# The first 256 tokens in two parts of 128, and the last silu in two halves with GpSimd beside VectorE

## The chip, the cores and the metric

The kernel runs on one core of a Trainium2 chip. The core has five engines that each work through their own queue in order: TensorE (PE in the profile; its weight loads are listed as PEld), VectorE (DVE), ScalarE (ACT), GpSimd (POOL) and SyncE (SP), which here only issues DMAs. They wait for each other through semaphores. The metric is the device time of one execution in microseconds (us), as the median of several runs. The kernel before takes 820.97 us (median of 3 runs, 820.76 to 821.0).

## What is computed

All is float32. `x` has 4 sequences of 1024 tokens, each token with 1024 features: 4096 rows. The reference, cut to what matters here:

```python
xn = _layernorm(x)                                   # per token: (x - mean) / sqrt(var + eps)

# first branch: a gate, and a recurrence along the sequences
g   = sigmoid(xn @ gate_w.T + gate_b)
u_g = xn * g
d_eff = d + mean_over_tokens(u_g) @ d_lr_u @ d_lr_v / rank
s   = c * decayed_cumsum(b * u_g) + d_eff * u_g

# second branch: three layers, and the top 2 of 8 routes
route = top2(softmax(xn @ wr.T))
h = silu(xn @ w1.T)
h = silu(h @ w3.T)
h = h @ w2.T
out = zeros_like(xn)
for k in range(2):
    out = out.at[index[:, k]].add(gate[:, k] * h)    # index is a route: rows 0 to 7 alone
g = silu(out)

return x + s * g
```

The rows that routes are added to are only rows 0 to 7 of `out`; silu of zero is zero, so all rows of the result but the first eight are `x` itself. The eight rows need a sum over all tokens of `h`, weighted by the gates, which is why all three big products (w1, gate_w for the first tokens, w3) are computed and w2 is applied once, at the very end, to the eight sums.

## The kernel before

**Tiles.** Tokens are taken in four super-blocks of 1024 (`sb`). For a super-block a product such as `xn @ w1.T` is a 1024 x 1024 x 1024 product. It is done as a 2 x 2 block product with seven block products in place of eight (a Strassen-Winograd scheme): the seven are numbered 1 to 7 and each of them is itself split once more in the same way into seven small products. A small product (`small`) is four matmuls with a 128 x 128 weight tile and 256 moving columns, accumulated in PSUM in two column halves. The class `Half` holds one of the block products, and its `step(n)` issues its n-th small product into one of the banks X, Z or Y and then has VectorE or ScalarE carry the bank into the result (`first`, `more`, `whole`). The kinds are "u" (w1), "g" (gate_w, only needed for the first super-block) and "m" (w3).

**The first product.** The first "u" product (line 211, `plain`) is done without the scheme: eight small products, two for each quarter of its result, since the sums that the scheme needs aren't there yet. The first "g" product uses the scheme. `at_first` (line 1438) says how the steps of the two are interleaved: steps 0 and 1 of "u" (bank X_u), then 0 and 3 of "g" (banks X_g and Y_g), then on with "u". These four small products need only the first 256 tokens of `xn`, the first half of the w1 block and the first half of the gate_w block.

**Normalisation of the first tokens.** `xT`, the transposed input, has features on the partitions, so mean and scale of a token have to lie along the free axis, the same on all partitions. `first_tokens` (line 317) takes the moments of tokens 0 to 255 from `x` itself (`x_first`, four pieces of 128 tokens by 512 features; VectorE's BN_STATS and BN_AGGREGATE), makes 128 x 128 diagonal matrices of the means (`spread(0, ...)`) and of the scales (`spread(1, ...)`), and multiplies them on TensorE by a matrix of ones, which puts each token's mean (bank mean_00) and scale (bank scale_00) on all partitions. `scales` computes the reciprocal root with one Newton step. Then `on` subtracts the mean and multiplies by the scale, on VectorE, straight in the tile of `xT`. `warm` issues matmuls on constants, whose results nobody reads, so that TensorE is at work meanwhile (`IDLE` of them ahead of everything). For the other quarters of the super-block (tokens 256 to 511 and so on) `stats0` and `norm0` do the same with larger operations; the mean and scale of tokens 256 to 511 go to bank acc.

**What sets the order.** Every engine instruction is pinned to the order in which the program issues it. This order is written by hand as places on a line: `at(place, f)` puts a function at a place, a generator may `yield` a distance to its next part, and before each small product at its place all that is due by then is issued. So a changed place moves instructions relative to those of the same engine, TensorE's queue among them: `stats0(0, 1, ..., 11.9, apart=1)` at place -8 puts the matmuls for mean and scale of tokens 256 to 511 at 3.9 and 4.9, between small products at 3, 4 and 5.

**DMAs.** All loads of the start go through SP's queue but two pieces of `x_first`, which ACT issues. The order on SP: two pieces of x, the first xT piece, the first half of w1's block, the second xT piece, the first half of gate_w's block, then x for tokens 256 to 511, the second halves, the rest of xT. Each DMA uses one of eight semaphores in turn; a DMA waits until the one eight before it has landed.

**The end.** After the last product, `the_rest` sums the last gated rows, transposes them, multiplies them by w2 into bank pp (32 partitions for each of four groups of 256 features, of which 8 rows are used), and then applies silu on ScalarE, multiplies by `y` and adds `x` on VectorE, each as one instruction of 128 x 256, and stores four pieces of 8 x 256, two by SP and two by ACT.

Of the kernel before, what the change touches and what calls it, by code (L numbers as in the profile page):

```python
# [10 lines left out]
F32 = mybir.dt.float32  # L11
I32 = mybir.dt.int32
U32 = mybir.dt.uint32
AF = mybir.ActivationFunctionType
# [8 lines left out]
def kernel(  # L23
# [99 lines left out]
                self.home.append(self.tile)  # L123

    NB, NQ = 20, 18
    IDLE = 14
    blocks = deque(
        const.tile([P, 4, 2 * Q], F32, tag=f"b{i}", name=f"b{i}") for i in range(NB)
    )
# [18 lines left out]
    pool.memset(three_halves, 1.5)  # L148

    x_first = block()  # L150
    for n in range(2):
        for t, queue in ((0, sync), (1, act)):
            queue.dma_start(
                x_first[:, 2 * t + n, :], x[t * P : (t + 1) * P, n * H : (n + 1) * H]
            )

    root = const.tile([P, 1], F32, tag="root", name="root")
    act.activation(root, eps, AF.Sqrt)
# [83 lines left out]
    def part(t, a):  # L242
        return t[:, 2 * a : 2 * a + 2, :].rearrange("p b (k n) -> p (b k) n", n=Q)
# [3 lines left out]
    def stats0(I, a, xb, lag, wait=(0, 0), apart=0):  # L247

        mv = sp.tile([P, 2, 2], F32, tag="mv", name=f"mv_{I}{a}")
        for tt in range(2):  # L250
            xt = xb[:, 2 * tt : 2 * tt + 2, :]
            bn = sp.tile([P, 2, nc.vector.BN_STATS_DIM], F32, tag=f"bn{tt}", name=f"bn_{I}{a}{tt}")
            for n in range(2):
                dve.bn_stats(bn[:, n, :], xt[:, n, :])
            dve.bn_aggr(mv[:, tt, :], bn)
        xb.drop()
        dg = quarter()

        def diagonals(s, w):
            for tt in range(2):  # L260
                act.activation(
                    dg[:, (2 * s + tt) * P : (2 * s + tt + 1) * P],
                    ident,
                    AF.Identity,
                    scale=w[:, tt : tt + 1],
                )

        if (I, a) == (1, 1):
            bc = ps_sm.tile([P, 2, Q], F32, tag="sm", name="bc_11")
        elif (I, a) == (1, 0):  # L270
            bc = ps_y.tile([P, 2, Q], F32, tag="Y", name="bc_10")
        else:
            bc = acc.rearrange("p (s n) -> p s n", s=2)
        yield wait[0]

        sd, v, r1 = (bc[:, 1, 2 * i : 2 * i + 2] for i in range(3))
        act.activation(sd, mv[:, :, 1], AF.Sqrt, bias=eps)
        act.activation(v, mv[:, :, 1], AF.Identity, bias=eps)
        diagonals(0, mv[:, :, 0])
        r0 = sp.tile([P, 2], F32, tag="r2", name="r0")  # L280
        rs = sp.tile([P, 2], F32, tag="rs", name=f"rs_{I}{a}")
        dve.reciprocal(r0, sd)
        dve.reciprocal(r1, sd)
        dve.scalar_tensor_tensor(rs, r0, -0.5, r1, ALU.mult, ALU.mult)
        dve.tensor_mul(rs, rs, v)
        dve.scalar_tensor_tensor(rs, rs, 1.5, r1, ALU.add, ALU.mult)
        yield wait[1]
        diagonals(1, rs)
        yield lag
        for s in range(2):  # L290
            if s:
                yield apart
            pe.matmul(
                bc[:, s, :],
                ones,
                dg[:, s * Q : (s + 1) * Q],
                start=True,
                stop=True,
                skip_group_check=True,
            )  # L300
            bc0[I, a] = [bc[:, s, :] for s in range(2)]
        dg.drop()

    def norm0(I, a, J, apart=0):
        p = part(xn[0, I, J], a)
        for s, op in ((0, ALU.subtract), (1, ALU.mult)):
            if s and apart:
                yield apart
            row = bc0[I, a][s].unsqueeze(1).to_broadcast([P, 4, Q])
            dve.tensor_tensor(p, p, row, op)  # L310

    def warm(n):

        for _ in range(n):
            pe.matmul(idle, ones, ident, start=True, stop=True, skip_group_check=True)

    def first_tokens():


        mv = sp.tile([P, 2, 2], F32, tag="mv", name="mv_00")  # L320
        bn = [
            sp.tile([P, 2, nc.vector.BN_STATS_DIM], F32, tag=f"bn{t}", name=f"bn_00{t}")
            for t in range(2)
        ]
        for n in range(2):
            for t in range(2):
                dve.bn_stats(bn[t][:, n, :], x_first[:, 2 * t + n, :])
        for t in range(2):
            dve.bn_aggr(mv[:, t, :], bn[t])
        x_first.drop()  # L330
        sd = sp.tile([P, 2], F32, tag="sd2", name="sd_00")
        act.activation(sd, mv[:, :, 1], AF.Sqrt, bias=eps)
        dg = quarter()
        rows = [
            ps_acc.tile([P, Q], F32, tag="rows", name="mean_00"),
            ps_sm.tile([P, Q], F32, tag="sm", name="scale_00"),
        ]
        bc0[0, 0] = rows

        def spread(s, w):  # L340
            d = dg[:, s * Q : (s + 1) * Q]
            for t in range(2):
                dve.tensor_scalar(
                    d[:, t * P : (t + 1) * P], ident, w[:, t : t + 1], None, ALU.mult
                )
            pe.matmul(rows[s], ones, d, start=True, stop=True, skip_group_check=True)

        spread(0, mv[:, :, 0])
        warm(2)
        v = sp.tile([P, 2], F32, tag="v2", name="v_00")  # L350
        dve.tensor_scalar(v, mv[:, :, 1], EPS, None, ALU.add)
        rs = sp.tile([P, 2], F32, tag="rs", name="rs_00")
        scales(rs, v, sd, 2)
        spread(1, rs)
        dg.drop()
        warm(3)
        p = part(xn[0, 0, 0], 0)

        def on(lo, hi, s, op):
            row = rows[s].unsqueeze(1).to_broadcast([P, hi - lo, Q])  # L360
            dve.tensor_tensor(p[:, lo:hi, :], p[:, lo:hi, :], row, op)

        on(0, 2, 0, ALU.subtract)
        on(0, 1, 1, ALU.mult)
        on(1, 2, 1, ALU.mult)
        on(2, 4, 0, ALU.subtract)
        on(2, 4, 1, ALU.mult)

    def stats(sb, bcs):

# [219 lines left out]
    def first_sums(t):  # L590

        for _ in fresh_sums("g", 1, t, False):
            yield 0.5
        yield 3
        for _ in left_sums("u", 0, 1, 1):
            yield 0.5

# [313 lines left out]
    class Half:  # L911
# [33 lines left out]
        def step(self, n):  # L945
# [16 lines left out]
            elif n == 0:  # L962
                go(self.X, A[:, 0], t[:, 0], True, False)
                self.first(0, self.X)
            elif n == 1:
                go(self.Z, s[0].tile, ts[0].tile, True, False)
                self.first(3, self.Z)
                s[0].drop()
                ts[0].drop()
            elif n == 2:  # L970
                go(self.X, s[1].tile, ts[1].tile, False, False)
                self.first(1, self.X)
                s[1].drop()
                ts[1].drop()
            elif n == 3:
                Y = ps_y.tile([P, 2 * Q], F32, tag="Y", name=f"Y_{self.tag}")
                go(Y, A[:, 1], t[:, 2], True, True)
                if (self.kind, self.i) == ("g", 1):
                    at(Y_AT, self.more, 0, Y)
                else:  # L980
                    self.more(0, Y)
            elif n == 4:
                go(self.X, s[2].tile, ts[2].tile, False, False)
                self.more(3, self.X)
                s[2].drop()
                ts[2].drop()
            elif n == 5:
                go(self.Z, s[3].tile, t[:, 3], False, True)
                self.more(1, self.Z)
                s[3].drop()  # L990
            elif n == 6:
                go(self.X, A[:, 3], ts[3].tile, False, True)
                self.first(2, self.X)
                self.whole(2)
                ts[3].drop()
# [237 lines left out]
    sync.dma_start(first[:, 0, :], xT[0, 0, 0, :, 0, :])  # L1233
    first_half("w1", 0)
    sync.dma_start(first[:, 1, :], xT[0, 0, 0, :, 1, :])
    first_half("gw", 0)
    load_x0(0, 1)
    first_half("w1", 1)
# [7 lines left out]
    at(-16, load_xn, 0, 1, 0, USES[1, 0] + G[1, 0])  # L1246
    at(-15, load_xn, 0, 1, 1, USES[1, 1] + G[1, 1])
    at(-10, first_tokens)
    at(-8, lambda: stats0(0, 1, x0[0, 1], 11.9, apart=1))
    at(3.95, norm0, 0, 1, 0, 1)  # L1250
    at(6, lambda: stats0(1, 0, x0[1, 0], 2.5, (1.5, 1)))
    at(6.5, norm0, 0, 0, 1)
    at(8.5, norm0, 0, 1, 1)
# [4 lines left out]
    at(18, norm0, 1, 1, 1)  # L1258
    at(26, consts)
    for IJ in HB:  # L1260
        at(0, lambda IJ=IJ: left.__setitem__(("u", 0, IJ), xn[(0,) + IJ]))

    halves = []
    for kind, sb, i, plain in line:
# [117 lines left out]
    def the_rest():  # L1382
# [36 lines left out]
            dve.tensor_add(accT[:, 4 + 2 * b : 6 + 2 * b, 0:E], ta[:, ks, :], half[:, ks, :])  # L1419
            part_out((4 + 2 * b, 5 + 2 * b), False, b == 0)  # L1420
        o = fin["o"]
        act.activation(o, p, AF.Silu)
        dve.tensor_mul(o, o, fin["y"])
        dve.tensor_add(o, o, fin["x"])
        for w in range(4):
            (sync, act)[w % 2].dma_start(
                out[0:E, w * Q : (w + 1) * Q], o[CG * w : CG * w + E, :]
            )

# [13 lines left out]
        (at_first[kind, sb, i][n] if (kind, sb, i) in at_first else start[kind, sb, i] + 2 * n, k, n)  # L1443
        for k, (kind, sb, i, plain) in enumerate(line)
        for n in range(8 if plain else 7)
    )
    for place, k, n in steps:
        here[0] = place
# [81 lines left out]
```

## Time and profile before

| what | value |
|---|---|
| median of 3 runs | 820.97 us (820.76 to 821.0) |
| the profiled execution | 820.79 us |
| its span, first to last instruction | 819.0 us |
| PE busy | 811.4 us (99%), 4087 matmul records |
| DVE, ACT, POOL busy | 510.6, 267.3, 496.5 us |
| mean granted TensorE clock | 0.999 |
| DMA moved | 192.88 MB, mean 235 GB/s |
| first matmul of X_u | 10.32 us |
| last matmul of pp ends | 814.81 us |

The span runs from the first to the last instruction; what lies around it (1.8 us) is in the time of the execution and not in the profile. All instructions that go through the class `Pinned` are listed under its line 89, so the profile is read by the names of the tiles: `X_u<-b,b` is a matmul that writes bank X_u of a "u" product from two large tiles, `q` is a tile of 128 x 512, `b` one of 128 x 2048, `bn` and `mv` are moments. A name followed by "q" (SPq, ACTq) is the engine's queue, here the issuing of a DMA. Busy shares are averages over the whole span: the start up to 10 us and the tail from 805 us are a small part of them.

### The profile page before, as it was taken

How to read it: one execution, taken by the hardware profiler on the slowest of the kernel's cores; microseconds unless marked ns; L12 is line 12 of the kernel's file. 1: busy time of each engine (PE TensorE's matmuls, PEld its weight loads, DVE VectorE, ACT ScalarE, POOL GpSimd, SP SyncE). 2: the span in 40 equal slices, each digit the busy share in tenths (PEclk: the TensorE clock that was granted, in tenths of full speed). 3: DMA queues.
4: the chain of work that ended last, by engine and by line, in shares of the span. 5: the costliest groups of instructions: out<-in, count | busy, mean ns of one | idle time of the engine just before them, and what ended most of it. 6: DMA issues, size and time to landing. Idle time of an engine off the chain costs nothing.

```text
span 819.0 us, 11323 instructions
## 1 busy us (share of the span) xinstructions
PE 811.4 (99%) x4087; PEld 698.2 (85%) x4087; DVE 510.6 (62%) x872; ACT 267.3 (33%) x470; POOL 496.5 (61%) x398
## 2 busy tenths in 40 slices
PE   8999999999999999999999999999999999999997
PEld 7888888888888878888888788888888788888885
DVE  6986598765588534764985235666983246667643
ACT  2345126877233237341022065421122021220111
POOL 2799796957999394644547453754448454465300
PEclk9999999999999999999999999999999999999999
DMA  9946609464978958629955866559766355555700
GB/s 341 423 169 232 231 27 359 180 244 152 409 275 311 339 183 295 246 88 380 387 170 221 334 224 238 193 206 385 282 244 241 120 213 207 197 177 178 302 14 2
DMA packets 55927, 192.88 MB, mean 235 GB/s; under 512 B 6480, under 2 KB 9792, under 8 KB 44224
## 3 DMA queue, kind: packets, MB, share of 16 engines
q1 hardware_dynamic: 55552, 191.61, 63.6%
q8 instruction: 33, 0.54, 0.2%
q10 hardware_dynamic: 320, 0.54, 0.2%
q14 instruction: 22, 0.18, 0.1%
HBM read 169.01 MB, written 39.87 MB: 255 GB/s over the span
## 4 chain that ended last, share of the span: by engine, by line
PE 98%; DMA 1%; DVE 0%; issue 0%; SPq 0%; ACT 0%
PE X_u L89 24%; PE X_m L89 24%; PE Z_u L89 12%; PE Z_m L89 12%; PE Y_m L89 6%; PE X_g L89 6%; PE Y_u L89 6%; PE Z_g L89 3%; PE acc L89 2%; PE plT L89 2%; PE Y_g L89 1%; DMA b<-in_x 1%; PE pp L89 0%; PE bc L89 0%; DVE bn L89 0%; PE accB L89 0%
## 5 line engine op out<-in xcount | busy, mean ns | idle before, releaser
L89 POOL TENSOR_TENSOR q<-b 128x512 f32<-128x512 f32 x154 | 203.5, 1336 | 194.6 <-PE X_m L89 48.0
L89 ACT ACTIVATE b<-b 128x512 f32<-128x512 f32 (+1 forms) x152 | 105.4, 696 | 296.5 <-DVE b L89 292.5
L89 POOL TENSOR_TENSOR q<-b,q 128x512 f32<-128x512 f32 x98 | 133.7, 1368 | 7.2 <-issue 4.0
L89 POOL TENSOR_TENSOR b<-b,b 128x512 f32<-128x512 f32 x72 | 93.1, 1318 | 48.5 <-PE X_u L89 33.8
L89 DVE TENSOR_TENSOR b<-b,b 128x512 f32<-128x512 f32 x120 | 109.2, 924 | 2.7
L89 PE MATMUL X_m<-q,q 128*128 128x256 f32 x448 | 105.9, 379 | 0.0
L89 PE MATMUL X_u<-q,q 128*128 128x256 f32 x432 | 102.4, 380 | 0.0
L89 DVE TENSOR_TENSOR b<-X_u,b 128x512 f32<-128x512 f32 x87 | 60.1, 691 | 58.6 <-PE X_u L89 57.9
L89 DVE TENSOR_TENSOR b<-X_m,b 128x512 f32<-128x512 f32 x88 | 60.3, 687 | 56.9 <-PE X_m L89 56.6
L89 PEld LDWEIGHTS X_m<-q,q 128*128 128x128 f32 x448 | 85.0, 190 | 12.4 <-issue 0.8
L89 POOL TENSOR_TENSOR q<-q,b 128x512 f32<-128x512 f32 x56 | 73.7, 1317 | 32.3 <-PE X_u L89 25.1
L89 PEld LDWEIGHTS X_u<-q,q 128*128 128x128 f32 x432 | 81.8, 190 | 12.2 <-issue 1.2
L89 DVE TENSOR_TENSOR b<-b,bc 128x1024 f32<-128x1024 f32 x56 | 67.8, 1210 | 0.1
L89 PE MATMUL X_u<-b,b 128*128 128x256 f32 x248 | 58.4, 379 | 0.0
L89 PE MATMUL Y_m<-b,b 128*128 128x256 f32 x224 | 53.1, 380 | 0.0
L89 PE MATMUL Z_m<-b,q 128*128 128x256 f32 x224 | 53.0, 379 | 0.0
L89 PE MATMUL X_m<-b,b 128*128 128x256 f32 x224 | 52.9, 379 | 0.0
L89 PE MATMUL Z_m<-q,q 128*128 128x256 f32 x224 | 52.9, 379 | 0.0
L89 PE MATMUL X_m<-q,b 128*128 128x256 f32 x224 | 52.9, 379 | 0.0
L89 PEld LDWEIGHTS X_u<-b,b 128*128 128x128 f32 x248 | 47.0, 190 | 6.4
L89 DVE TENSOR_TENSOR b<-Z_u,b 128x512 f32<-128x512 f32 x47 | 32.5, 691 | 31.6 <-PE Z_u L89 30.9
L89 PE MATMUL Z_u<-q,q 128*128 128x256 f32 x216 | 51.1, 379 | 0.0
(182 smaller groups left out, 1179.2 us busy)
## 6 DMA issues: line engine op xcount, KB each, us to landing
q<-w SPq DMA_DIRECT2D x168, 256.0 KB, 4.5
b<-in_w SPq DMA_DIRECT2D x36, 1024.0 KB, 8.8
b<-w_T SPq DMA_DIRECT2D x24, 1024.0 KB, 6.2
b<-in_xT SPq DMA_DIRECT2D x15, 1024.0 KB, 11.6
w<-q SPq DMA_DIRECT2D x56, 256.0 KB, 7.1
b<-in_x SPq DMA_DIRECT2D x12, 1024.0 KB, 10.9
w_T<-b SPq DMA_DIRECT2D x8, 1024.0 KB, 4.4
b<-in_gw SPq DMA_DIRECT2D x6, 1024.0 KB, 15.6
```

The source lines that it names most:

```text
L89: r = f(*args, **kwargs)
```

## The change

The first 256 tokens are handled in two parts of 128, each with its own moments, spreading, row operations and the four small products with 128 moving columns in place of 256; the DMAs of `x` are reordered so that the pieces of tokens 0 to 127 come first (one on SP, one on ACT) and those of tokens 128 to 255 later on SP; the diagonals of the means and the sum of variance and eps move from VectorE to ScalarE. The matmuls for mean and scale of tokens 256 to 511 and the row operations on them move by one place, and the second of the row operations is halved. At the end the silu is done in two halves of 128 columns, GpSimd multiplies and adds for the first and VectorE for the second, and of the four stores SP issues two, ACT one and GpSimd's queue one. The diff, cut (removed bodies of `first_tokens` are left out, they stand in the listing above; `urgent` is never set):

```diff
-    IDLE = 14
+    IDLE = 12
...
-    for n in range(2):
-        for t, queue in ((0, sync), (1, act)):
-            queue.dma_start(
-                x_first[:, 2 * t + n, :], x[t * P : (t + 1) * P, n * H : (n + 1) * H]
-            )
+    def first_piece(queue, t, n):
+        queue.dma_start(x_first[:, 2 * t + n, :], x[t * P : (t + 1) * P, n * H : (n + 1) * H])
+
+    first_piece(sync, 0, 0)
+    first_piece(act, 0, 1)
...
     def norm0(I, a, J, apart=0):
-            row = bc0[I, a][s].unsqueeze(1).to_broadcast([P, 4, Q])
-            dve.tensor_tensor(p, p, row, op)
+            n = 2 if s and apart else 4
+            row = bc0[I, a][s].unsqueeze(1).to_broadcast([P, n, Q])
+            for k in range(0, 4, n):
+                dve.tensor_tensor(p[:, k : k + n], p[:, k : k + n], row, op)
...
     def first_tokens():
+        def moments(t):
+            for n in range(2):
+                dve.bn_stats(bn[t][:, n, :], x_first[:, 2 * t + n, :])
+            dve.bn_aggr(mv[:, t, :], bn[t])
+            act.activation(sd[:, t : t + 1], mv[:, t, 1:2], AF.Sqrt, bias=eps)
+            act.activation(diagonal(0, t), ident, AF.Identity, scale=mv[:, t, 0:1])
+            act.activation(v[:, t : t + 1], mv[:, t, 1:2], AF.Identity, bias=eps)
+            o = slice(t, t + 1)
+            scales(rs[:, o], v[:, o], sd[:, o], 1)
+            dve.tensor_scalar(diagonal(1, t), ident, rs[:, o], None, ALU.mult)
...
+        hu.begin()
+        hg.begin()
+        moments(0)
+        spread(0, 0)
         warm(2)
+        spread(1, 0)
+        warm(2)
+        Y = ps_y.tile([P, 2 * Q], F32, tag="Y", name="Y_g0_1")
+        four = (
+            (hu.X, 0, hu.t[:, 0], True, False),
+            (hu.X, 1, hu.t[:, 2], False, True),
+            (hg.X, 0, hg.t[:, 0], True, False),
+            (Y, 1, hg.t[:, 2], True, True),
+        )
+        on(0, 2, 0, 0)
+        on(0, 1, 0, 1)
+        on(1, 2, 0, 1)
+        on(2, 4, 0, 0)
+        on(2, 4, 0, 1)
+        for n, (ps, q, B, start, stop) in enumerate(four):
+            half_small(ps, hu.A[:, q], B, 0, start, stop)
+            if n == 0:
+                moments(1)
+        x_first.drop()
+        spread(0, 1)
+        spread(1, 1)
         dg.drop()
+        for k in range(4):
+            for s in range(2):
+                on(k, k + 1, 1, s)
+        for ps, q, B, start, stop in four:
+            half_small(ps, hu.A[:, q], B, 1, start, stop)
+        at(3.9, hu.first, 0, hu.X)
+        at(3.9, hg.first, 0, hg.X)
+        at(Y_AT, hg.more, 0, Y)
...
-        yield 3
+        yield 3.6
         for _ in left_sums("u", 0, 1, 1):
...
     sync.dma_start(first[:, 1, :], xT[0, 0, 0, :, 1, :])
+    first_piece(sync, 1, 0)
+    first_piece(sync, 1, 1)
     first_half("gw", 0)
...
-    at(-8, lambda: stats0(0, 1, x0[0, 1], 11.9, apart=1))
-    at(3.95, norm0, 0, 1, 0, 1)
+    at(-8, lambda: stats0(0, 1, x0[0, 1], 12.9, apart=1))
+    at(4.96, norm0, 0, 1, 0, 1)
...
-        at(0, lambda IJ=IJ: left.__setitem__(("u", 0, IJ), xn[(0,) + IJ]))
+        at(-11, lambda IJ=IJ: left.__setitem__(("u", 0, IJ), xn[(0,) + IJ]))
...
         o = fin["o"]
-        act.activation(o, p, AF.Silu)
-        dve.tensor_mul(o, o, fin["y"])
-        dve.tensor_add(o, o, fin["x"])
+        for n, eng in ((0, pool), (1, dve)):
+            c = slice(n * P, (n + 1) * P)
+            act.activation(o[:, c], p[:, c], AF.Silu)
+            eng.tensor_mul(o[:, c], o[:, c], fin["y"][:, c])
+            eng.tensor_add(o[:, c], o[:, c], fin["x"][:, c])
         for w in range(4):
-            (sync, act)[w % 2].dma_start(
+            (sync, act, pool)[w % 3].dma_start(
                 out[0:E, w * Q : (w + 1) * Q], o[CG * w : CG * w + E, :]
             )
...
         for n in range(8 if plain else 7)
+        if not (k == 0 and n in (0, 1) or k == 1 and n in (0, 3))
```

In the new `first_tokens`, `on(lo, hi, t, s)` is the row operation (s = 0 subtracts the mean, s = 1 multiplies by the scale) on rows `lo` to `hi` of the tile and on part t, `spread(s, t)` is the 128-column matmul with the matrix of ones, and `half_small` issues the four matmuls of `small` with the 128 columns of part t. The last line takes the four steps, which `first_tokens` now issues itself, out of the list of steps.

More of the change, by code (lines that the diff above doesn't have):

```diff
@@ L257, in stats0, with diagonals @@
         dg = quarter()
-        def diagonals(s, w):
+        def diagonals(s, w, urgent=False):
             for tt in range(2):
[L261 to L266, printed above, removed]
+                d = dg[:, (2 * s + tt) * P : (2 * s + tt + 1) * P]
+                if urgent:
+                    dve.tensor_scalar(d, ident, w[:, tt : tt + 1], None, ALU.mult)
+                else:
+                    act.activation(d, ident, AF.Identity, scale=w[:, tt : tt + 1])
         if (I, a) == (1, 1):
@@ L278, in stats0 @@
         act.activation(v, mv[:, :, 1], AF.Identity, bias=eps)
-        diagonals(0, mv[:, :, 0])
+        diagonals(0, mv[:, :, 0], False)
         r0 = sp.tile([P, 2], F32, tag="r2", name="r0")
@@ L317, in first_tokens @@
     def first_tokens():
-        mv = sp.tile([P, 2, 2], F32, tag="mv", name="mv_00")
         bn = [
@@ L324, in first_tokens @@
         ]
[L325 to L330, printed above, removed]
+        mv = sp.tile([P, 2, 2], F32, tag="mv", name="mv_00")
         sd = sp.tile([P, 2], F32, tag="sd2", name="sd_00")
-        act.activation(sd, mv[:, :, 1], AF.Sqrt, bias=eps)
+        v = sp.tile([P, 2], F32, tag="v2", name="v_00")
+        rs = sp.tile([P, 2], F32, tag="rs", name="rs_00")
         dg = quarter()
@@ L338, in first_tokens @@
         bc0[0, 0] = rows
[L340 to L348, printed above, removed]
-        warm(2)
-        v = sp.tile([P, 2], F32, tag="v2", name="v_00")
-        dve.tensor_scalar(v, mv[:, :, 1], EPS, None, ALU.add)
@@ L352, in first_tokens @@
-        rs = sp.tile([P, 2], F32, tag="rs", name="rs_00")
-        scales(rs, v, sd, 2)
-        spread(1, rs)
-        dg.drop()
[L356 to L367, printed above, removed]
+        p = part(xn[0, 0, 0], 0)
@@ new lines, in first_tokens, with diagonal @@
+        hu, hg = halves[0], halves[1]
+        def diagonal(s, t):
+            n = s * Q + t * P
+            return dg[:, n : n + P]
+        def moments(t):
[8 more added lines that the diff above has]
+            dve.tensor_scalar(diagonal(1, t), ident, rs[:, o], None, ALU.mult)
@@ new lines, in spread, with on @@
+        def spread(s, t):
+            pe.matmul(
+                rows[s][:, t * P : (t + 1) * P],
+                ones,
+                diagonal(s, t),
+                start=True,
+                stop=True,
+                skip_group_check=True,
+            )
+        def on(lo, hi, t, s):
+            c = slice(t * P, (t + 1) * P)
+            row = rows[s][:, c].unsqueeze(1).to_broadcast([P, hi - lo, P])
+            op = (ALU.subtract, ALU.mult)[s]
+            dve.tensor_tensor(p[:, lo:hi, c], p[:, lo:hi, c], row, op)
@@ new lines, in half_small @@
+        def half_small(ps, A, B, t, start, stop):
+            for mt in range(2):
+                for kt in range(2):
+                    n = kt * Q + t * P
+                    pe.matmul(
+                        ps[:, mt * Q + t * P : mt * Q + (t + 1) * P],
+                        B[:, kt * Q + mt * P : kt * Q + (mt + 1) * P],
+                        A[:, n : n + P],
+                        start=(start and t == 0 and mt == 0 and kt == 0),
+                        stop=(stop and t == 1 and mt == 1 and kt == 1),
+                        skip_group_check=True,
+                    )
@@ new lines, in first_tokens @@
+        hu.begin()
+        hg.begin()
+        moments(0)
+        spread(0, 0)
+        warm(2)
+        spread(1, 0)
[6 more added lines that the diff above has]
+            (Y, 1, hg.t[:, 2], True, True),
+        )
+        on(0, 2, 0, 0)
+        on(0, 1, 0, 1)
+        on(1, 2, 0, 1)
+        on(2, 4, 0, 0)
@@ L977, in step @@
                 go(Y, A[:, 1], t[:, 2], True, True)
[L978 to L981, printed above, removed]
+                self.more(0, Y)
             elif n == 4:
```

## The prediction

> **What bounds the kernel now.** I read the chain of waits first, for the whole run (its shares by engine, the first line below) and then in order of time for its first 45 us (start, length, work): it says which work sets the end.
>
> ```profile
> PE 98%; DMA 1%; DVE 0%; issue 0%; SPq 0%; ACT 0%
> ...
> 1.20 4.66 DMA b<-in_x
> 5.86 0.02 issue
> 5.88 1.29 DVE bn L89 x2
> ...
> 9.80 0.67 PE idle L89 x6
> 10.47 3.57 PE X_u L89 x16
> ```
>
> PE is the bound from the first X_u to the tail. Between 10.3 and 813.7 us the trace has no moment in which PE stands still, so a microsecond won or lost at the start arrives at the end whole. Ahead of X_u stand the landing of x, the moments on DVE, and the spreading of mean and scale. Next the timeline of PE and of DVE (start, length, engine, what, and in brackets the idle time before and who ended it), whose starts I use as the price list; PE has two records for a matmul:
>
> ```profile
> 9.64 0.83 PE L89 MATMUL idle<-ident,ones 128*128 128x128 f32 x6
> 10.32 3.72 PE L89 MATMUL X_u<-b,b 128*128 128x256 f32 x16
> 13.88 1.89 PE L89 MATMUL X_g<-b,b 128*128 128x256 f32 x8
> 17.33 0.59 PE L89 MATMUL acc<-q,ones 128*128 128x256 f32 x2
> 17.76 1.89 PE L89 MATMUL Z_u<-b,b 128*128 128x256 f32 x8
> 19.49 0.59 PE L89 MATMUL acc<-q,ones 128*128 128x256 f32 x2
> 19.92 1.89 PE L89 MATMUL Z_u<-b,b 128*128 128x256 f32 x8
> 21.64 3.62 PE L89 MATMUL X_u<-b,b 128*128 128x256 f32 x16
> ```
>
> A 256-column matmul costs 0.432 (8 in 3.46). A 128-column one costs 0.223: idle records start 0.111 apart. After a wait PE's second record starts 0.32 after the first instead of 0.216, so each stop costs 0.1 on top. Last the tail, in the timelines by engine, with one POOL/DVE pair from before it:
>
> ```profile
> 778.37 1.27 POOL L89 TENSOR_TENSOR q<-b,q 128x512 f32<-128x512 f32 x1 [3.96 <-issue]
> 778.99 1.19 DVE L89 TENSOR_TENSOR b<-b,b 128x512 f32<-128x512 f32 x1
> ...
> 814.87 0.38 ACT L89 ACTIVATE b<-pp 128x256 f32<-128x256 f32 x1 [4.83 <-PE pp L89]
> 815.29 0.88 DVE L89 TENSOR_TENSOR b<-b 128x256 f32<-128x256 f32 x2 [1.61 <-ACT b L89]
> 816.20 0.66 SPq L89 DMA_DIRECT2D out<-b  x2
> 816.21 0.97 ACTq L89 DMA_DIRECT2D out<-b  x2
> ```
>
> **First part, tokens 0 to 127: X_u 1.9 earlier.** Only two of the four x pieces are needed. The first still lands at 4.52 and bn starts at 4.54. The second bn runs 5.16 to 5.83, the aggregate ends at 6.02, ACT's sqrt at 6.33 (0.27 to 0.30 by its rows). ACT then makes the mean diagonal and v (starts 0.20 and 0.29 apart, as at 15.31, 15.51, 15.80), so v is there at 6.82. DVE's reciprocal starts at 6.37; its three dependent steps are 0.20 apart, the second held by v to 6.85 (behind it only the rest of this chain); the scale diagonal ends at 7.53. From the scale matmul to the multiply took 0.73 with 256 columns; 0.21 less with 128. The multiply starts at 8.10 and takes 0.29 (rows: 0.28 for a 128 TENSOR_SCALAR, 0.42 for 256 columns). X_u starts at 8.42 instead of 10.32.
>
> **Then PE waits for weights: about 0.4.** X_u's eight half matmuls end at 10.35. X_g needs gw's first half. In the semaphore events of before, w1's half landed at 8.71, the second xT piece at 9.40 and gw's half at 10.75. The change leaves the same 2 MB ahead of gw (the x pieces go from ACT's queue into SP's), so 10.75 stays; two more SP issues of 0.4 before gw's are covered, as gw's issue at 3.48 lay seven microseconds ahead of its landing, and the loads queued behind it on SP wait for landings anyway. Behind the waiting X_g stands all of PE's queue, the second spreads first. The other end is 10.1: w1's half took 2.0 where gw's took 1.35, in a stretch with the DMA share at 0.74 to 0.85, and this loss need not come back. X_g starts at 10.79, and it and Y_g end at 12.67 (8 x 0.223 + 0.1).
>
> **Second part: PE waits for DVE.** DVE comes to the new bn pair at 9.3, ends it at 10.56 and needs 1.5 from aggregate to scale diagonal as above: 12.27, hidden behind PE's 12.67. The two spread matmuls then take 0.45 on PE with nothing behind them but X_u, and X_u needs rows that DVE can start only now: eight operations of 128 columns, of which a subtract and its multiply cost 0.52 together. Rows 0 to 3 are done at 13.7, 14.22, 14.74 and 15.26. PE stops for rows 0, 1 and 3, ends X_u at 16.07 and Y_g at 17.85 (8 x 0.223). Before, Y_g ended at 17.33. The lead of 1.9 has become a lag of 0.52.
>
> **The acc matmuls move behind Z_u: about 1.05.** The shift of stats0 and norm0 by one place gives Z_u, acc, Z_u, acc, X_u instead of acc, Z_u, acc, Z_u, X_u; the built order shows it. The sum on PE is the same 4.31, but Z_u no longer covers DVE's multiply by the scale. The second acc starts at 17.85 + 1.73 + 0.43 + 1.73 = 21.74 and ends at 22.34; half the multiply (128x512, 0.69; the change halves it) ends at 23.06, and X_u starts at 23.1 plus 0.1 for the stop. Before: 21.64. Lag 1.56. The same rows put the old Z_u at 17.61 where it came at 17.76; three more stops make such misses likelier, so I take 1.7. Late next are POOL's sums (they wait for this multiply), but Z_g, which uses the first, came 4 us after it: covered, as are the places 3.6 and -11. IDLE 12 ends the idle matmuls at about 6.0 instead of 6.3, before the mean: nothing.
>
> **Tail: 0.05.** Half a silu is about 0.26 (0.38 for 256 and 0.63 for 512 columns): ends 815.13 and 815.30. POOL has no 128-column row: a quarter of 1.27 is 0.32, the whole 1.27; I take 0.39, from its memsets' 0.1 fixed part. The pair shown tells that the two engines don't overlap: DVE's SBUF add took 1.19 beside POOL's and 0.69 alone, ending 0.54 after it. So the four run in turn: POOL to 815.56, DVE to 815.85, POOL to 816.24, DVE to 816.53, against 816.17 before (815.98 were they free). In return the last issue falls away: ACT's pair takes 0.97, SP's 0.66, so 0.31 back. Sum 0.36 - 0.31 = 0.05, if POOL's DMA lands by SP's second. Before has no POOL DMA. Lower end: an ACT issue, 1.5 from issue to landing, hidden. Upper end: the program's first transfer, 0.74 to 4.52, 3.8, which adds 2.2. Nearest is the ACT row, also a queue long unused, so I count nothing and keep 2.2 for the range.
>
> The Trainium skill speaks against both tail edits. "SBUF — State Buffer", section "SBUF: two separate sides", has the port pair of GpSimd and VectorE as an exclusive lock held for the whole instruction, also for a VectorE operation with two SBUF inputs; the 1.19 row agrees, and without the rule the tail would be -0.5. "DMA: Bandwidth & Descriptors", section "Anatomy of one DMA — SWDGE (gpsimd) path", gives about 2.0 us fixed for a transfer from GpSimd; no run here shows it yet, and by it the tail would be an estimated +0.35 rather than +0.05.
>
> **Sum.** The profiled execution took 820.79 with a span of 819.0; 1.7 + 0.05 makes 822.55, and the median stands 0.18 above that execution: **822.7**.
>
> **Rivals.** The 0.2% that a measurement of this kernel can tell is 1.64: slower begins above 822.61, faster below 819.33.
>
> A, the lead survives, not slower: PE doesn't wait for the eight row operations. Without the gw and row stops Y_g ends at 16.2, 1.65 sooner: 821.0; with the acc wait and the port wait gone too, 1.05 and 0.55 less: 819.5, so that a third of the case falls below 819.33. It decides where the second scale diagonal is ready some 2 us ahead of PE; against it, its x lands at 9.4 and the chain behind it is 5.9 long. Chance 0.11.
>
> B, gw early at 10.1: 0.59 off, 822.1. For it the full DMA share from 8.5 on. 0.13.
>
> C, POOL's DMA lands late: from 0.3 up to 2.2 more, 823.0 to 824.9. For it, a queue never used before; against, only 8 KB. 0.26.
>
> Forecast: 0.50, own range 822.0 to 823.4, about two thirds of it above 822.61.
>
> **Numbers.** Slower: 0.32 of the forecast, 0.26 of C, 0.04 of B: 0.62. Same: 0.18 + 0.09 + 0.07 of A: 0.34. Faster: 0.04. The range leaves out most of A below and the last of C above: 821.5 to 824.3.
>
> **What would show it.** X_u at 8.4; X_g waiting for gw near 10.8; three stops in the second X_u; Z_u at 17.9; X_u behind the second acc with a gap of 0.9; DVE and POOL taking turns at the tail. Wrong, if Z_u starts before 17.0, or the second acc isn't followed by a gap; the sum of the tail, if the last output waits for POOL's queue.

## The result, and the profile after

The changed kernel takes 824.34 us (median of 5 runs, 824.25 to 824.97) against 820.97 (5 runs, 820.62 to 821.08): a ratio of 1.0043, with a 95% interval of 1.0032 to 1.0054. It is slower by 3.37 us. The forecast was 822.7 with a range of 821.5 to 824.3, so the direction was right and the size too small: the median lies 0.04 above the range's upper end. The profiled execution took 824.34 with a span of 822.58, against 820.79 and 819.01 before.

The difference of the two spans, 3.56 us, has two places. The start first: TensorE's timeline of the changed kernel from 8 us on (start, length, engine, operation; in brackets how long the engine had stood still before it, and what ended that).

```profile
8.23 1.16 PE L89 MATMUL X_u<-b,b 128*128 128x128 f32 x8
9.71 1.16 PE L89 MATMUL X_u<-b,b 128*128 128x128 f32 x8 [0.32 <-DVE b L89]
11.67 1.16 PE L89 MATMUL X_g<-b,b 128*128 128x128 f32 x8 [0.80 <-DMA b<-in_gw]
12.66 1.06 PE L89 MATMUL Y_g<-b,b 128*128 128x128 f32 x8
13.55 0.39 PE L89 MATMUL mean<-q,ones 128*128 128x128 f32 x2
13.78 0.39 PE L89 MATMUL scale<-q,ones 128*128 128x128 f32 x2
14.71 1.46 PE L89 MATMUL X_u<-b,b 128*128 128x128 f32 x8 [0.55 <-DVE b L89]
...
18.83 1.89 PE L89 MATMUL Z_u<-b,b 128*128 128x256 f32 x8
20.65 0.67 PE L89 MATMUL acc<-q,ones 128*128 128x256 f32 x2
21.15 1.89 PE L89 MATMUL Z_u<-b,b 128*128 128x256 f32 x8
22.88 0.59 PE L89 MATMUL acc<-q,ones 128*128 128x256 f32 x2
24.30 3.69 PE L89 MATMUL X_u<-b,b 128*128 128x256 f32 x16 [0.83 <-ACT b L89]
27.83 0.38 PE L89 MATMUL Z_u<-b,b 128*128 128x256 f32 x1
```

VectorE's work ahead of the last of these stops, and, from the kernel before, the group at which both are compared:

```profile
23.51 1.28 DVE L89 TENSOR_TENSOR b<-b,acc 128x512 f32<-128x512 f32 x2 [0.34 <-PE acc L89]
...
25.10 1.89 PE L89 MATMUL Z_u<-b,b 128*128 128x256 f32 x8
```

X_u starts 2.09 us earlier than the 10.32 of before, and what follows eats more than that. There are four stops: rows that wait for the second xT piece (0.32), X_g for gate_w's first half (0.80), the second part's rows (0.55), and X_u behind the second acc (0.83); and from the second mean to the second X_u, 13.55 to 14.71, TensorE has but two spreading matmuls to do. The last stop names ACT, whose copy had ended by 23.66; what came last is VectorE's multiply by the scale, the first of two halves, 23.51 to 24.20. The third Z_u group comes at 27.83 against 25.10: 2.73 us late. From there to the end of the last pp matmul both kernels take the same, 789.7 us.

The tail of the changed kernel, from its last pp matmuls on:

```profile
816.48 1.07 PE L89 MATMUL pp<-b,accT 128*32 128x256 f32 x16 [0.27 <-DVE accT L89]
817.62 0.45 ACT L89 ACTIVATE b<-pp 128x128 f32<-128x128 f32 x2 [4.83 <-PE pp L89]
817.97 0.99 POOL L89 TENSOR_TENSOR b<-b 128x128 f32<-128x128 f32 x2 [35.59 <-ACT b L89]
818.10 1.01 DVE L89 TENSOR_TENSOR b<-b 128x128 f32<-128x128 f32 x2 [1.67 <-ACT b L89]
819.17 0.66 SPq L89 DMA_DIRECT2D out<-b  x2
819.18 0.62 ACTq L89 DMA_DIRECT2D out<-b  x1
819.75 0.70 POOL L89 DMA_DIRECT2D out<-b  x1 [0.79 <-DVE b L89]
```

From the end of the last pp matmul (817.55) to the end of the span is 5.02 us; before it was 4.21 (814.81 to 819.01). GpSimd's store starts 0.58 after SP's first and, by its semaphore, lands at 821.51, when ACT's and SP's second have been down since 820.68 and 820.88. The last landing is 3.96 us behind the last pp matmul, where before ACT's second store landed 3.36 behind it (818.17): 0.60 of the tail's 0.81. The rest is what the engines do behind the last landing, 1.06 for 0.85. So 2.73 + 0.81 = 3.54 us are found, all but 0.02 of the span's growth. The chain of the profile's page, which named PE with 98% before, is of no use here (`DVE 0%; POOLq 0%; issue 0%`). It follows the last landing back to GpSimd's queue and breaks off in the last microseconds: a chain of 0% is one that the profile could not follow.

### The profile page after: what moved, and what is told of

It is laid out like the page before. It is cut to its first block, busy times and chain, and to the rows that moved or that the text cites. A ratio compares the mean times of both kernels' runs of the same rounds, so it can differ in the third digit from the quotient of the medians.

```text
span 822.6 us, 11409 instructions
## 1 busy us (share of the span) xinstructions
PE 812.8 (99%) x4117; PEld 700.4 (85%) x4117; DVE 511.9 (62%) x882; ACT 268.8 (33%) x476; POOL 497.7 (61%) x401
## 5 line engine op out<-in xcount | busy, mean ns | idle before, releaser
L89 PE MATMUL X_u<-b,b 128*128 128x256 f32 (+1 forms) x264 | 59.5, 369 | 1.7 <-DVE b L89 0.9
```

Source lines behind the costliest of these rows:

```text
L89: r = f(*args, **kwargs)
```

## The experiments

Each is one of the two kernels with a small edit, or, for `after_b` and `after_c`, without one. All are read at the same marks: the landings of the first loads (semaphore events), the starts of X_g and of the third Z_u group (25.10 before), and the tail as defined above. Where a ratio is given, it is to runs of the kernel before on the same chip, whose medians were 820.79 to 820.81.

**Start and tail apart.** `front_only` is the changed kernel with the tail of before; `tail_only` is the kernel before with the tail of the change.

> The changed start with the tail of before. Theory (start and tail add up, and nothing between them gives time back): the third Z_u starts at 27.8 as in the changed kernel, 2.7 later than before, the tail from the last pp matmul to the end of the span takes 4.2 again, and the time is 820.97 + 2.7 = 823.7. Rival (part of the loss lies in the middle, or the start's loss is noise of that run): the time differs from 823.7 by over 0.5.

> The start of before with the changed tail. Theory (GpSimd's DMA lands last): GpSimd's store starts about 0.6 after SP's first and lands 0.6 after SP's second; the tail from the last pp matmul to the end is 5.05 instead of 4.2, and the time is 820.97 + 0.85 = 821.8. Rival (the tail costs only what the shared port costs, as the prediction's sum had it): 821.0 to 821.2.

Measured: 823.70, 1.0033 [1.0021, 1.0045], third Z_u at 28.05, tail 4.18; and 821.82, 1.0012 [1.0003, 1.0021], third Z_u at 25.19, tail 5.05. By the marks the start costs 2.95 and the tail 0.84, 3.79 in all; 0.22 of it is that X_g in `front_only` started at 11.89 and not at 11.67, and the remaining 3.57 is, within 0.01, the growth of the change's whole span. So the two parts do not touch each other. By medians they cost 2.91 and 1.03, 3.94 against 3.37 for the change; that the start differs between executions by as much as this excess is shown below, and so the marks carry the sum.

**The tail's two edits apart.**

```diff
 tail_compute: before, with
-        act.activation(o, p, AF.Silu)
-        dve.tensor_mul(o, o, fin["y"])
-        dve.tensor_add(o, o, fin["x"])
+        for n, eng in ((0, pool), (1, dve)):
...
 tail_store: before, with
-            (sync, act)[w % 2].dma_start(
+            (sync, act, pool)[w % 3].dma_start(
```

> The kernel before with only the last silu's halves and the GpSimd multiplies beside VectorE; the stores stay on SP's and ACT's queues. Theory: GpSimd and VectorE take turns, so that the data is done about 0.2 us later after the projection's end than before (1.55 against 1.36), the tail is 4.4 against 4.2, the time 821.0 (+0.2). Rival, that the shared multiplies cost the tail its whole 0.84 us: tail 5.0, time 821.6.

> The kernel before with its own silu and VectorE multiplies; only one of the last stores goes by GpSimd's queue. Theory: that store starts some 0.6 us after SP's and lands some 0.6 after SP's second, and the tail ends by it: 4.2 + 0.6 = 4.8, the time 821.4 to 821.6. Rival, that the queue is no slower than ACT's and the multiplies carry the loss: tail 4.2, time 820.8.

Measured: 820.98, 1.0002 [0.9993, 1.0011], tail 4.43 (the theory's 4.4); and 821.15, 1.0003 [0.9994, 1.0012], tail 4.44. By times alone neither differs from before; by the tails each costs 0.23, and both together 0.84. Of the missing 0.38, 0.31 stands in the start of GpSimd's store, here in `tail_store`:

```profile
815.32 0.89 DVE L89 TENSOR_TENSOR b<-b 128x256 f32<-128x256 f32 x2 [1.61 <-ACT b L89]
816.23 0.66 SPq L89 DMA_DIRECT2D out<-b  x2
...
816.50 0.68 POOL L89 DMA_DIRECT2D out<-b  x1 [36.84 <-DVE b L89]
```

An idle GpSimd starts its store 0.27 after SP's first; in the change, where it has itself just multiplied and added, 0.58 after. `tail_only` (0.58 too) and `tail_store` differ only in the silu's halves and in who multiplies and adds, so the 0.31 comes with that work; what GpSimd does in it the profile does not show. From start to landing it is 1.76 to 1.79 us in all three. The expectation for the store alone (0.6 more) was too high since it took over the 0.58. Besides, the span ends 0.99 after the last landing in `tail_store`, 1.06 in `tail_only` and in the change, against 0.85 before, so that of the 0.23 of `tail_store` only 0.08 is a later landing. It is 0.95 in `three_sp` below, which has no store from GpSimd; why the closing instructions take longer is open.

**The shift of the acc matmuls alone.** `shift_only` and `shift2` are the kernel before with the changed places; the second also takes over the change's later place of a GpSimd sum.

```diff
-    at(-8, lambda: stats0(0, 1, x0[0, 1], 11.9, apart=1))
-    at(3.95, norm0, 0, 1, 0, 1)
+    at(-8, lambda: stats0(0, 1, x0[0, 1], 12.9, apart=1))
+    at(4.96, norm0, 0, 1, 0, 1)
...
 shift2 too:
-        yield 3
+        yield 3.6
```

> Before, with the matmuls for mean and scale of tokens 256 to 511 one place later, norm0 at 4.96 and its second operation halved, all else as before. Theory (PE has to wait for a scale that stands right ahead of X_u): the second acc comes at about 21.2, X_u at 22.6 instead of 21.64 after a stop of about 0.8, and the time is 0.95 to 1.05 more, 821.9 to 822.0. Rival (the halves and PE's queue hide it): under 0.3 more, 821.2 at most.

> The kernel before with the second part's lag and halved normalisation of the change, and with the left sum issued behind the multiply as in the change. Theory: the third X_u group's stop is 0.8 to 0.9 us instead of 1.27, and the third Z_u starts 0.95 to 1.05 later than in the kernel before, time 821.8. Rival, that the lag costs what the earlier run with the same lag showed whatever the sum's place: +1.6, time 822.5.

Measured: 822.63, 1.0033 [1.0022, 1.0043], third Z_u at 26.71 (+1.61); and 821.79, 1.0011 [1.0002, 1.0020], third Z_u at 26.16 (+1.06). In `shift_only` the sum is issued ahead of the multiply by the scale, so it adds rows that are not yet scaled, and the multiply waits for it. VectorE's and TensorE's timelines of `shift_only`:

```profile
22.39 1.28 DVE L89 TENSOR_TENSOR b<-b,acc 128x512 f32<-128x512 f32 x2 [0.78 <-POOL q L89]
...
23.18 3.69 PE L89 MATMUL X_u<-b,b 128*128 128x256 f32 x16 [1.26 <-issue]
```

and of `shift2`:

```profile
22.63 3.69 PE L89 MATMUL X_u<-b,b 128*128 128x256 f32 x16 [0.83 <-ACT b L89]
...
21.84 1.28 DVE L89 TENSOR_TENSOR b<-b,acc 128x512 f32<-128x512 f32 x2 [0.34 <-PE acc L89]
```

The stop of 0.83 is that of the changed kernel to the hundredth, and the price, 1.06, is the forecast's 1.05. The first expectation, 0.95 to 1.05 for `shift_only`, missed because it did not see that the 3.6 belongs to the shift: the wait for GpSimd's sum (0.78) made the stop 1.26. Three of the eight runs of `shift_only` took 824.6 to 825.23, and its ratio counts them; the profiled one took 822.42, so what these three waited for is not shown.

**The change without the shift.** `noshift` is the changed kernel with 11.9, 3.95 and 3, and the row operation whole.

> The changed kernel with the second part's lag and whole normalisation of the kernel before. Theory: with the first part in two, TensorE would wait for the mean's diagonal block right after the second gate group, so that the lag was the lesser evil: the third X_u group no earlier than 24.3, time 824.3 to 824.9. Rival, that the lag's price comes back when the lag is taken out: X_u about 0.9 earlier, time 823.4.

Measured: 824.99, 1.0048 [1.0034, 1.0061], third Z_u at 28.81, a microsecond later than with the shift.

```profile
18.26 1.06 PE L89 MATMUL Y_g<-b,b 128*128 128x128 f32 x8
20.97 0.67 PE L89 MATMUL acc<-q,ones 128*128 128x256 f32 x2 [1.65 <-DVE rs L89]
```

TensorE stands for 1.65 us right behind Y_g, as VectorE, held up by the second part's rows, comes to the statistics of tokens 256 to 511 only now: their first pair starts at 16.45, before it was 12.05. So the shift is a price of the two parts, not a separable mistake. The expectation had the sign and place; the loss came out at 25.36 - 24.30 = 1.06 at X_u, of which this execution's later gw (11.94 against 11.62) explains 0.3. By the medians the loss is 0.65.

**Why gw lands late.** The first theory was that x's second part, moved from two queues into one, slows the loads. `pieces_act` issues it from ACT in the changed kernel; `sp_only` does the reverse, all x on SP in the kernel before.

> The changed kernel, with the two x pieces of tokens 128 to 255 issued by ACT's queue instead of SP's (behind its first piece). Theory (one hardware queue alone does not keep the 16 engines at work in this stretch, two do): the DMA share between 4 and 8 us stays at 0.9 or more, gw's first half lands by 10.9 instead of 11.62, and the time falls by 0.6 to 0.9, to 823.4 to 823.7. Rival (the transfer of w1's half is slow by itself, on whatever queue the others are): a dip to 0.75 or less wherever w1's half moves, gw at 11.3 or later, and the time within 0.3 of 824.3.

> The kernel before with all four pieces of the first 256 tokens on SP's queue; the order and the bytes of all loads stay. Theory: one queue alone moves the first loads more slowly, so that the first half of gw lands near 11.6 us as in the changed kernel instead of 10.75; nothing waits for it here (X_g starts at 13.9), so the time stays at 820.8 to 821.1 unless x itself lands later. Rival: gw lands at 10.7 to 10.9, and its lateness in the changed kernel comes from something else than the queue that x takes.

Measured: gw at 10.64 in `pieces_act` (823.91, 1.0038 [1.0024, 1.0051]). That landing fits the theory and the rest does not: the DMA share fell to 0.63 and 0.62 between 4.5 and 5.5 us, and the time fell by 0.43, less than the 0.6 that was the least expected, since X_u now waited for w1's half (8.62) and X_g started only at 11.24. In `sp_only` (821.49, 1.0010 [1.0001, 1.0019]) gw came at 11.17, which fits neither side, and the time is 0.68 longer with gw awaited by nothing. Its profile (822.26) has the loss behind the third Z_u, which at 24.96 is not late: VectorE waits 2.40 us for an xT piece, to 27.02, where the same operation began at 24.92 before, and the bc matmuls that start at 36.32 before start at 37.11. Put beside the other runs, gw's landing is no wonder: in the eight profiles in which the first loads are exactly those of the kernel before, gw's half landed at 10.52, 10.75, 10.79, 11.18, 11.26, 11.42, 11.78 and 12.21. That is a second theory, spread, and it was put to the test by profiling two kernels again without any edit.

> The changed kernel itself, profiled again. Theory: when gw lands differs from execution to execution (10.5 to 12.2 us in the eight profiles in which these loads are those of the kernel before), here anywhere between 10.4 and 12.1, and TensorE follows it: X_g 0.05 after the landing but not before 10.9, the third Z_u 16.2 after X_g. Rival: one queue for the second part's x makes gw late every time: 11.5 to 12.0.

> The changed kernel itself, profiled a third time. Theory and rival as for the second: gw anywhere between 10.4 and 12.1 with the third Z_u 16.2 after X_g, against 11.5 to 12.0 every time.

> The changed kernel with the second part's x on ACT's queue, profiled again. Theory: gw's landing of 10.64 in its first profile was one draw from the same spread; here anywhere between 10.4 and 12.1. Rival: with x on two queues gw lands at 10.5 to 10.8 in this kernel every time.

> The same kernel profiled a third time. Theory: gw anywhere between 10.4 and 12.1; rival: 10.5 to 10.8.

| kernel | w1's half lands | gw's half lands | X_g starts | third Z_u | profiled time |
|---|---|---|---|---|---|
| change | 7.84 | 11.62 | 11.67 | 27.83 | 824.34 |
| `after_b` | 6.97 | 11.19 | 11.24 | 27.40 | 823.97 |
| `after_c` | 6.94 | 10.98 | 11.03 | 27.18 | 823.75 |
| `pieces_act` | 8.62 | 10.64 | 11.24 | 27.30 | 823.85 |
| `pieces_act_b` | 9.48 | 11.51 | 12.10 | 28.16 | 824.71 |
| `pieces_act_c` | 9.55 | 11.58 | 12.17 | 28.23 | 824.79 |

The rival falls: with one queue gw also comes at 10.98, with two also at 11.58. The third Z_u stands 16.15 to 16.16 behind X_g in the three executions of the change and 16.06 in the three of `pieces_act`, where X_g has no stop in front of it, and the times differ by what X_g differs by, within 0.1. TensorE in `after_c`:

```profile
8.06 2.23 PE L89 MATMUL X_u<-b,b 128*128 128x128 f32 x16
11.03 1.16 PE L89 MATMUL X_g<-b,b 128*128 128x128 f32 x8 [0.73 <-DMA b<-in_gw]
```

and in `pieces_act_b`:

```profile
9.62 1.13 PE L89 MATMUL X_u<-b,b 128*128 128x128 f32 x8 [1.44 <-DMA b<-in_w]
11.10 1.16 PE L89 MATMUL X_u<-b,b 128*128 128x128 f32 x8 [0.36 <-DVE b L89]
12.10 1.06 PE L89 MATMUL X_g<-b,b 128*128 128x128 f32 x8
```

In the second, X_u itself waits, for w1; X_g then finds gw there. Whichever load comes last, TensorE now follows it. (This spread is in the times too: 823.75 to 824.97 for the changed kernel over all runs.)

But the spread is not shown to be one between executions alone, for the runs were made on several chips. The landings of gw's half by chip:

| chip | loads of before | loads of the change | x's second part by ACT |
|---|---|---|---|
| not recorded | 10.75 | 11.62 | |
| 15 | 10.52, 10.79 | 11.85 (`front_only`) | 10.64 |
| 2 | 11.18, 11.26, 11.42 | 11.94 (`noshift`) | |
| 10 | | 10.98, 11.19 | 11.51, 11.58 |
| 11 | 11.78, 12.21 | | |

On one chip and with one order of loads the values lie within 0.07 to 0.43 of each other; most of the 1.7 us is between chips. In the rows that have both, the change's loads bring gw 0.5 to 1.3 later. So a rival stands, that the new order of loads itself costs time. Against it speaks chip 11, where `sp_only` had gw at 11.17 and `gw_ahead` (below) all of the same 2.5 MB at 11.27, both earlier than the loads of before there; and ACT's queue is the faster one on chip 15 and the slower one on chip 10. No run has both orders several times on one chip, so how much of the 0.87 between 10.75 and 11.62 is the order and how much is the draw stays open.

**gw ahead of x.** In the changed kernel, `first_half("gw", 0)` is put ahead of the two pieces of the second part.

> The changed kernel with the first half of gw ahead of the second part's pieces of x on SP's queue. Theory: gw lands at 10.3, X_g's stop of 0.80 goes, but the second part's x lands 1.34 later, and the wait moves to its statistics: the second scale starts near 14.1 instead of 13.8, the third Z_u at 28.1, time 824.6. Rival, that gw's landing is the only price of the order of loads: the third Z_u 0.8 earlier, at 27.0, time 823.5.

Measured: 824.34, 1.0045 [1.0031, 1.0059]; gw lands at 9.91, the last piece of x at 11.27.

```profile
10.55 1.06 PE L89 MATMUL X_g<-b,b 128*128 128x128 f32 x8
...
12.90 0.49 PE L89 MATMUL mean<-q,ones 128*128 128x128 f32 x2 [0.40 <-ACT q L89]
13.79 0.49 PE L89 MATMUL scale<-q,ones 128*128 128x128 f32 x2 [0.41 <-DVE q L89]
14.66 1.56 PE L89 MATMUL X_u<-b,b 128*128 128x128 f32 x9 [0.38 <-DVE b L89]
```

X_g starts 1.12 us earlier and the second X_u at 14.66 instead of 14.71: the gain is gone after two groups, to the second part's statistics. The third Z_u is at 27.78 (27.83), not at the rival's 27.0; the theory's 28.1 was 0.3 too late, since the loads came sooner than in the execution it was worked out from.

**Is something to be had over the kernel before?** `three_sp` sends the last four stores as SP, ACT, SP, SP; `best3` adds the second scale diagonal on ACT.

```diff
-            (sync, act)[w % 2].dma_start(
+            (sync, act, sync, sync)[w].dma_start(
...
 best3 too, in spread:
+                if s and t:
+                    act.activation(d[:, P:Q], ident, AF.Identity, scale=w[:, 1:2])
+                else:
```

> The kernel before with its last four stores three on SP's queue and one on ACT's instead of two and two. Theory: SP issues one every 0.36 us, ACT the second only 0.67 after the first, so that SP's third starts at about the same time as ACT's second did; the last lands 0.2 earlier at most: tail 4.0 to 4.2, time 820.6 to 820.8. Rival: a third store on one queue lands later, tail 4.4, 821.0.

> The kernel before with the three stores on SP's queue, and at the start the second scale diagonal block by ACT beside VectorE's first. Theory: the scale matmul starts 0.15 to 0.2 earlier (8.9 instead of 9.1), X_u at 10.15, and as TensorE does not stop after it, the lead lasts: time 820.4 to 820.6. Rival: ACT's hop takes what VectorE's second block took, and nothing moves: 820.6 to 820.8.

Measured: 820.92, 1.0001 [0.9992, 1.0010], tail 4.34; and 821.24, 1.0003 [0.9994, 1.0012], tail 4.34. SP's third store starts no earlier than ACT's second did (2.10 and 2.07 after pp's end), so nothing is gained; by the marks the tail is 0.13 longer. In `best3` the scale matmul came 0.17 earlier (8.94 for 9.11), but in the profiled execution w1's half landed only at 10.20, and X_u started at 10.33: the landing took the gain. In these two executions the loads came so late (gw at 11.78 and 12.21) that VectorE waited 1.1 and 1.2 us for the x of tokens 256 to 511, and the third Z_u came at 25.49 and 25.90: late loads can cost the kernel before too. Neither is an improvement that these runs could tell, and no version beat the kernel before.

## Why the prediction fell short

The steps of the prediction against the profile, in its order:

- *X_u starts 8.42 instead of 10.32.* 8.23, and 8.05 and 8.06 in the two other executions; 8.79 and 8.47 in `front_only` and `noshift`, which have the same start. Right.
- *"The change leaves the same 2 MB ahead of gw ..., so 10.75 stays."* This is the step that failed. gw landed at 11.62, X_g started at 11.67 and not at 10.79: 0.88 us. The bytes were the same, but 10.75 was a single value: eight profiles of the same loads give 10.5 to 12.2 with a middle of 11.2, five of the changed order of loads (the three of the change, `front_only`, `noshift`) 10.98 to 11.94 with a middle of 11.6. Whether the new order or the draw made the 0.87 is open, as said above; equal bytes ahead of gw did not make an equal landing. The kernel before cannot show what gw's landing costs, since its X_g comes at 13.88, behind every landing in that spread. And the bound was one-sided: 10.1 as the early end, no late end at all.
- *X_g and Y_g take 1.88 more, then DVE's rows.* From X_g to the second mean 1.88 was measured; from there to Z_u 5.28 for 5.18. Right.
- *The acc matmuls behind Z_u cost 1.05.* `shift2` measured 1.06 by itself. Right, with the mechanism; and `noshift` showed that leaving them in their old place would have cost some 0.67 more (28.81 less 27.83 at the third Z_u, less the 0.31 by which its X_g started later).
- All the steps behind X_g together: 16.16 us to the third Z_u, where the forecast's numbers make 10.79 + 16.01 = 25.10 + 1.7. Off by 0.15.
- *Tail 0.05, "so I count nothing and keep 2.2 for the range".* The tail cost 0.81. The turns of GpSimd and VectorE were there, at 0.19 instead of 0.36 (data done 1.56 after pp's end against 1.37), as the VectorE operation ends 0.15 after GpSimd's and not a full length after it. The prediction's own pair had this already: VectorE's 1.19 ended 0.54 after GpSimd's, and not the 0.69 that it takes alone. GpSimd's store is what was set at nothing, without a row for it: rival C's mechanism, inside its bounds. It starts late (0.58) and lands 0.63 after SP's second. The row taken as nearest, an ACT issue, was of the wrong engine, and the multiplies on the issuing engine made it later still. Of the 0.81, 0.60 is the later landing and the rest lies behind it, which no term had.

The sum: 0.88 for gw's landing, 0.15 for the steps behind it and 0.76 for the tail make 1.79; less 0.18, by which the forecast placed the median above the profiled execution, 1.61, against the 1.64 that 824.34 lies above 822.7. So the two large terms are both transfers, and both were sized by one row of another execution or another queue. The compute steps were right within 0.2. Whether an execution ends inside the range or 0.04 above it hangs on the landing: two single ones on another chip took 823.75 and 823.97.

Rival A, that the lead survives, is out: with gw at the earliest that the changed kernel showed, 10.98, the third Z_u comes at 27.18, 2.08 late. Rival B, an early gw, did occur: at 9.91 with another order of loads, where it changed nothing. The price of the two parts does not hang on gw's landing alone. Where X_g had no wait for gw, it followed the second half of X_u's matmuls by 0.99 (10.25 and 11.24 in `pieces_act`) and the third Z_u followed it by 16.06. That half started at 9.14 in `after_c` (the ninth of its 16 records) and at 9.71 in the change, so an estimate of the third Z_u without the wait for gw is 26.2 to 26.8, 1.1 to 1.7 later than before. It is a low one, as 16.06 need not stay: in `gw_ahead`, where X_g had no wait either, the second part's statistics made it 17.23.

The tail also bears on two rules of the Trainium skill. "DMA: Bandwidth & Descriptors", section "Anatomy of one DMA — SWDGE (gpsimd) path", has about 2.0 us fixed for a transfer from GpSimd. The runs agree when GpSimd was idle: in `tail_store` it was 2.08 us from the end of VectorE's last operation to the landing, 816.20 to 818.28, of which 1.78 from the store's start; behind its own multiplies it was 819.11 to 821.51, 2.40. "SBUF — State Buffer", section "SBUF: two separate sides", has the port pair as a lock for the whole instruction. The measured pair is in accord for most of an operation, but a 128-column VectorE operation beside GpSimd's took 0.48 to 0.50 in all and ended 0.15 after it, where 128-column rows without GpSimd beside them take 0.28 to 0.29 (other operations, none of them this one). So some 0.14 of it seems to run beside GpSimd's, as 0.15 of the 512-column one did; the profile's ends of GpSimd operations are rough.

## What to carry to other kernels

When an edit pulls an engine's start forward to where loads still land, the landing becomes the price: take it from several executions, and on several chips, and bound it on the late side, since a profile in which nothing waited for it shows one value. Before the first product is cut in parts, count what every later step then finds late: here 2.1 to 2.3 us of lead became 2.1 to 2.7 of lag within four groups of waits, and moving one load or one group moved the wait on to the next. And the last stores of this kernel are better left on SP's and ACT's queues: GpSimd's store started later than theirs, and later still when GpSimd had just computed.

## What the runs showed that was not expected

- The landings of the same first loads spread by more than 1 us between profiles, mostly from chip to chip, though the medians of the kernel before, 820.79 to 820.97, do not show it. In the eight profiles with the loads of before, x has landed by 5.9 to 6.3, the first xT piece at 6.7 to 8.2; gw's half then follows w1's by 2.00 to 2.04 every time. So the spread arises early, among the first transfers, and the later ones go at an even rate. What causes it is open; the choice of queue does not show as the cause, since its sign differs between two chips.
- A DMA issue from GpSimd takes 0.68 to 0.70 us, and starts 0.30 us after VectorE's last operation when GpSimd had been idle, 0.64 when it had just computed.
